# A fused attention and feed-forward block: x and x1 transposed by DVE after loads in 128-byte pieces, and score masks written as products of steps

## The chip, the core and the metric

The kernel runs on one core of a Trainium2 chip. TensorE (PE, with its weight loads shown apart as PEld), VectorE (DVE), ScalarE (ACT) and GpSimd (POOL) each run their own instruction list in order. SyncE (SP) issues nearly all transfers, in order too, and waits for the semaphores of each before it issues it. The metric is the device time of one execution in microseconds; the profiled execution gives a span, from the first instruction to the last, which is a little shorter than its time.

## What is computed

One block with the norm behind each part: x is 4096 rows of 256 values in fp32, `x1 = norm(x + attention(x))`, `out = norm(x1 + ffn(x1))`. Attention has 16 heads of 16 values in 4 groups that share keys and values, and a row sees itself and the 127 rows before it:

```python
scores = einsum('bghqd,bgkd->bghqk', q, k) / sqrt(16)
mask   = (i - 128 >= j) | (i < j)
att    = softmax(where(mask, -1e9, scores));  out = att @ v @ Wo + bo
# ffn, with x_prev = the row before
xr = mu_r * x + (1 - mu_r) * x_prev;  xk = mu_k * x + (1 - mu_k) * x_prev
out = sigmoid(xr @ W_r.T) * (square(relu(xk @ W_k.T)) @ W_v.T)
```

## The kernel before

The 4096 rows are cut into blocks of 128, pairs of blocks (p = 0 to 15, 256 rows each) and chunks of two pairs (c = 0 to 7, 512 rows).

**How the order is made.** Every stage is an operation given to `op(...)` with its kind, what it reads and writes, which buffers of a ring (a pool of a few tiles in turn) and which of the eight PSUM banks it takes. The table `KINDS` gives each kind its engine, an assumed length in microseconds and a rank. `Plan.run` then plays the operations through: each engine takes, among the operations that could start within a small window (`WAIT`, for PE `PE_WAIT`), the one of lowest rank plus `base`, which is about its pair's number. A change of the way that PE is cut into tiles (`mode`) is charged `TURN`; a transfer is counted as landed `LAND` after SP has issued it. The instructions of all engines are written out in the order that comes of this, so it is fixed when the program runs.

**The stages of a pair.**

- `plan_load` loads x of a pair (256 KB, 1 KB rows, ring of 4). `plan_xT` transposes it on PE by four 128x128 transposes (L560) and ACT copies the result from PSUM (L567).
- `plan_kv`, `plan_q` (per chunk; L583, L631) make kT and qT, each head group with spare rows beside its 16 values. `q move` (L653) is four transfers inside SBUF that shift half of qT, in pieces of 128 bytes; `ones` (L617) fills the spare row of kT. `plan_v` transposes the values (L606) and DVE copies them (L611).
- `plan_maxima`, in three units: first scores on PE with their masks (L695, L708), their negated maxima by DVE (L718), a small DVE transpose (L728), and `nm put` (L732), four transfers of 4 KB that place the maxima in the spare row of qT.
- `plan_weights_a` (per block) and `plan_weights_b` (per pair): second scores on PE, transposed, so that keys lie on partitions, with the maxima already subtracted (L787); before them their masks (L775); then exp by ACT (L827, L855). `half_scores` and `scores` build these. The masks are matmuls of a shifted identity (`intoE`, `intoO`, cut out of `identZ`) with `maskOwn`, `maskPrev` or, for the block before the first, `maskNone`. They set half of the 64 rows at a time: one half by a mask of one group of columns, the other half by a mask of two.
- `plan_values` (L882, L895) multiplies by the values; DVE turns, scales and turns back (L907 to L927).
- `plan_out`: xres is x loaded again (L1006) with bo added by POOL (L1012), `wo` on PE (L1021), the sum by DVE (L1031), then the norm: `stats` on DVE (L960), `scale` on POOL (L966 to L972), `apply` on ACT (L978). The result is x1 (ring of 6).
- `plan_x1T` transposes x1 on PE (L1054) and ACT copies it (L1067) into x1T, one column further right, the first column being the last of the pair before (L1064, POOL).
- `plan_mix`: POOL takes differences of neighbouring columns (xd, L1082), DVE mixes (xm, L1090). `plan_k`, `plan_r`, `plan_vout`: products fk (L1118), fr and fv (L1144), relu and tanh on ACT, square (L1132) and the sum with x1 (L1176) on POOL, the gate (L1171) on DVE, then the second norm and the store (L1182). The last pair ends in half pairs (`plan_last`).

`load_rest`, one operation, loads W_r, W_k, W_v, Wo and bo; the three W are transposed by PE once (`plan_weight`).

Of the kernel before, what the change touches and what calls it, by code (L numbers as in the profile page):

```python
# [20 lines left out]
P = 128  # L21
# [13 lines left out]
    "w": (PE, 0.43, -14.24),  # L35
    "w copy": (ACT, 0.62, 3.74),
    "x load": (SP, 0.5, -8.79),
    "x first": (SP, 3.3, -12.27),
    "x second": (SP, 2.5, -8.28),
    "xT": (PE, 0.43, 0.69),  # L40
    "xT copy": (ACT, 0.6, 5.02),
    "kv": (PE, 1.72, -6.04),
    "kv copy": (ACT, 0.69, -12.31),
    "vT": (PE, 0.43, -3.72),
    "vT copy": (DVE, 0.4, 1.8),
    "ones": (SP, 0.1, -12.06),
    "q": (PE, 1.72, -2.77),
    "q copy": (ACT, 0.69, -9.26),
    "q move": (SP, 2.0, -9.27),
    "maxima": (PE, 0.93, -1.84),  # L50
    "maxima 2": (PE, 0.66, -2.01),
    "reduce": (DVE, 1.14, 1.56),
    "reduce 2": (DVE, 0.81, -16.65),
    "nm turn": (DVE, 0.21, -6.03),
    "nm put": (SP, 2.0, 5.46),
    "weights a": (PE, 1.1, -0.52),
    "exp a": (ACT, 1.02, -9.82),
    "weights b": (PE, 1.3, -0.14),
    "exp b": (ACT, 1.02, 8.26),
    "values": (PE, 2.7, 0.67),  # L60
    "oN": (DVE, 1.25, -2.26),
    "rs": (DVE, 0.35, 9.56),
    "at": (DVE, 0.9, -0.26),
    "attT": (DVE, 0.44, 3.73),
    "xres": (SP, 0.5, -7.25),
    "bo": (POOL, 1.3, 19.18),
    "wo": (PE, 1.72, 2.61),
    "y": (DVE, 0.69, 9.88),
    "x1T first": (POOL, 0.25, 21.46),
    "x1T": (PE, 0.43, 3.16),  # L70
    "x1T copy": (ACT, 0.6, 10.29),
    "xd": (POOL, 1.3, -1.75),
    "xm": (DVE, 0.45, 27.04),
    "fk": (PE, 1.72, 6.41),
    "relu": (ACT, 0.6, 4.81),
    "square": (POOL, 1.07, 27.6),
    "fr": (PE, 1.72, 7.15),
    "gate": (ACT, 0.6, 13.52),
    "fv last": (PE, 0.86, 37.29),
    "y2 last": (DVE, 0.42, 26.45),  # L80
    "stats last": (DVE, 1.0, 21.07),
    "scale last": (POOL, 1.05, -29.88),
    "apply last": (DVE, 0.46, -15.48),
    "fv": (PE, 1.72, 3.74),
    "y2": (DVE, 0.69, -0.64),
    "y2 add": (POOL, 1.3, -4.68),
    "store": (SP, 0.5, -2.34),
    "rest": (SP, 4.5, 9.89),
    "stats y": (DVE, 0.6, 9.58),
    "scale y": (POOL, 1.5, 16.27),  # L90
    "apply y": (ACT, 0.6, 3.08),
    "stats y2": (DVE, 0.6, 10.75),
    "scale y2": (POOL, 1.5, -23.39),
    "apply y2": (ACT, 0.6, 23.42),
# [46 lines left out]
class Plan:  # L141
# [7 lines left out]
    WAIT = 0.39  # L149
    PE_WAIT = 0.20  # L150
    TURN = 0.2

    def __init__(self):
        self.ops = []
        self.writer, self.readers = {}, {}
        self.users, self.taker = {}, {}
        self.banks = Banks()

    def op(self, kind, base, fn, r=(), w=(), uses=(), new=(), banks=(), mode=None):
# [5 lines left out]
        rank += base  # L165
# [19 lines left out]
        self.ops.append((eng, length, rank, fn, deps, list(new), list(banks), mode))  # L185

    def run(self):
# [40 lines left out]
        while cand:  # L228
            best = {}
            for i in cand:  # L230
                s = ring_time(i)
                if s is None:
                    continue
                e = ops[i][0]
                s = max(ready[i], s, free.get(e, 0.0))
                places = None
                if ops[i][6]:
                    found = self.banks.find([k for _, k in ops[i][6]], free_at, s)
                    if found is None:
                        continue  # L240
                    s, places = found
                turn = self.TURN if e == PE and ops[i][7] != last_mode else 0.0
                best.setdefault(e, []).append((s + turn, i, places))
# [8 lines left out]
            eng, length, _, fn, _, new, banks, mode = ops[i]  # L252
# [8 lines left out]
            land = eng == SP  # L261
            free[e] = s + length
            end[i] = s + (self.LAND + length if land else length)
            order.append((s, len(order), i))
            for k in nexts[i]:
                hop = 0.0 if ops[k][0] == eng and not land else self.DRAIN if eng == PE else self.HOP
# [13 lines left out]
def postln_block(  # L280
# [45 lines left out]
    small = ctx.enter_context(tc.tile_pool(name="small", bufs=2))  # L326
    psum = ctx.enter_context(tc.tile_pool(name="psum", bufs=1, space=PSUM))
# [21 lines left out]
    def load_x(p):  # L349
# [4 lines left out]
        )  # L354

# [122 lines left out]
    identZ = const.tile([P, 3, Q], BF16, tag="identZ", name="identZ")  # L478
    nc.vector.memset(identZ, 0.0)
    nc.vector.tensor_copy(identZ[:, 1, :], identR[:, 0, :])  # L480
    intoE = identZ[:, 1:3, :].rearrange("p a b -> p (a b)")
    intoO = identZ[:, 0:2, :].rearrange("p a b -> p (a b)")


    nc.vector.tensor_tensor(diag, diag, after, ALU.add)
    four = diag.to_broadcast([P, GS, Q])
    maskOwn = const.tile([P, 2, GS, Q], BF16, tag="maskOwn", name="maskOwn")
    maskPrev = const.tile([P, 2, GS, Q], BF16, tag="maskPrev", name="maskPrev")
    nc.vector.memset(maskOwn[:, 0, :, :], NEG)
    nc.vector.memset(maskPrev[:, 1, :, :], NEG)  # L490
    nc.vector.tensor_scalar(maskOwn[:, 1, :, :], four, -NEG, NEG, ALU.mult, ALU.add)
    nc.vector.tensor_scalar(maskPrev[:, 0, :, :], four, NEG, None, ALU.mult)
    maskNone = const.tile([P, T], BF16, tag="maskNone", name="maskNone")
    nc.vector.memset(maskNone, NEG)
# [17 lines left out]
    def load_rest():  # L512
        for k, w in (("r", W_r), ("k", W_k), ("v", W_v)):
            load_w(ffn_l[k], w)
        for g in range(NG):
            nc.sync.dma_start(
                out=wo[32 * g : 32 * (g + 1), :, :],
                in_=Wo[64 * g : 64 * (g + 1), :].rearrange("(rp x) n -> x rp n", x=32),
            )
        nc.sync.dma_start(out=bo_b, in_=bo.partition_broadcast(P))  # L520
# [4 lines left out]
    def plan_weight(k, base, scale):  # L525
# [14 lines left out]
        op("w", base, turn, r=["rest"], w=[("wps", k)], banks=[(key, 1)], mode="full")  # L540
# [5 lines left out]
    def plan_load(p):  # L546
        if p > 1:
            op("x load", p, lambda: load_x(p), w=[("x", p)], new=[(ring("x", 4), ("x", p))])
# [3 lines left out]
    def plan_xT(p, base):  # L552
# [18 lines left out]

        op("xT", base, turn, r=[("x", p)], w=[key + ("ps",)], uses=[("x", p)] + ([("xTt", c)] if h else []),
# [184 lines left out]
    def scores(b, h, dst, own, r0, nr, first):  # L757

        c, blk = divmod(b, NB)
        k0 = (b + own) * P + 64 * h  # L760
        RQ = GS * Q
        if own:
            lo = (2 * h - r0) * RQ
            masks = ((intoE, maskOwn[:, 1:2], lo, 1), (intoO, maskOwn[:, 0:2], lo, 2))
        elif b == 0:
            masks = ((intoE, None, 0, nr), (intoO, None, 0, nr))
        else:
            lo = (2 * h - r0) * RQ
            masks = ((intoE, maskPrev[:, 0:2], lo, 2), (intoO, maskPrev[:, 0:1], lo + RQ, 1))

        def mask(i):
            into, m, lo, n = masks[i]
            for g in range(NG):
                q = slice(32 * g, 32 * (g + 1))
                nc.tensor.matmul(  # L775
                    dst[g][:, lo : lo + n * RQ],
                    into[q, :],
                    maskNone[q, 0 : n * RQ] if m is None else m[q].rearrange("p s r i -> p (s r i)"),
                    start=(i == 0 and first),
                    stop=False,  # L780
                    skip_group_check=True,
                )

        def product():
            for g in range(NG):
                k = slice(32 * g, 32 * g + DH + 1)
                nc.tensor.matmul(  # L787
                    dst[g],
                    kT[k, k0 : k0 + 64],
                    qT[c][k, blk, r0 : r0 + nr, :, :].rearrange("p s r i -> p (s r i)"),  # L790
                    start=False,
                    stop=True,
                    skip_group_check=True,
                )

        return mask, product

    def half_scores(b, sc, cols, kinds, first):
        parts = []
        for h in range(2):  # L800
            own, r0, nr = kinds[h]
            dst = [
                sc[g // 2][64 * h : 64 * (h + 1), g % 2, cols] for g in range(NG)
            ]
            parts.append(scores(b, h, dst, own, r0, nr, first))
        for i in range(2):
            for mask, _ in parts:
                mask(i)
        for _, product in parts:
            product()  # L810
# [6 lines left out]
    def plan_weights_a(b, base):  # L817
# [3 lines left out]
        def product():  # L821
            half_scores(b, [two_banks(k) for k in keys], slice(0, T), ((1, 0, NS), (0, 0, NS)), True)
# [14 lines left out]
    def plan_weights_b(p, base):  # L837
# [3 lines left out]
        def product():  # L841
            sc = [two_banks(k) for k in keys]
            for j in range(2):
                half_scores(
                    2 * p + j,
                    sc,
# [481 lines left out]
```

## Time and profile before

| | us |
|---|---|
| median of three runs | 356.84 (355.78 to 358.21) |
| the profiled execution | 357.12 |
| its span | 355.4 |
| DVE: maxima reduce (L718), 96 | 94.0 |
| DVE: mixing (L1090), 64 | 34.3 |
| ACT: exp (L827 and L855), 96 | 92.9 |
| ACT: copies of x1T and xT (L1067, L567), 32 | 18.2 |
| PE: transposes of x (L560), 64, and of x1 (L1054), 64 | 9.2 and 10.3 |
| PE: masks of second scores (L775), 1024 | 70.2, overlapping |

The busy time of a group is what its own instructions cover. PE runs several small matmuls side by side in parts of its array, so groups overlap and their times are not to be added up; the price of a stage is better read from the starts of the stages, one after the other. The rest of what matters is shown with the prediction.

### The profile page before, as it was taken

To read this page: it belongs to the slowest core of one execution; us is meant where nothing else is said; L and a number is where in the kernel's file an instruction comes from. 1 tells how busy PE (TensorE), PEld (TensorE's weight loads), DVE (VectorE), ACT (ScalarE), POOL (GpSimd) and SP (SyncE) were. 2 spreads that over 40 slices of the span, in tenths; PEclk is the share of its full clock that TensorE was granted. 3 is DMA by queue.
4 is the path that set the end of the run, shared out by engine and by line. 5 is a ranking of instruction groups with operands and counts; after the bars stand their busy time and mean duration, and the time that the engine had idled before them with its cause. 6 is when DMAs were issued, how large, how long until landed. Compare 5 with 4: busy or idle time off the path is not lost.

```text
span 355.4 us, 11751 instructions
## 1 busy us (share of the span) xinstructions
PE 342.9 (96%) x5091; PEld 230.2 (65%) x5091; DVE 244.8 (69%) x464; ACT 179.0 (50%) x253; POOL 125.8 (35%) x223
## 2 busy tenths in 40 slices
PE   6999999999999999999999999999999999999982
PEld 5655565566747676767657676766757676667871
DVE  4146474888593898988927987388845888548554
ACT  3423537273537284647355554737456373863441
POOL 5110000412234363534315251253505352626883
PEclk9989999999999999999999999999999999999997
DMA  6855150140004101102223020320205020200011
GB/s 187 260 88 77 50 92 5 32 64 5 8 29 34 61 33 33 50 16 58 66 21 73 5 61 5 31 61 4 63 3 83 16 60 5 61 4 0 31 59 60
DMA packets 34518, 17.34 MB, mean 49 GB/s; under 512 B 20734, under 2 KB 34434, under 8 KB 34466
## 3 DMA queue, kind: packets, MB, share of 16 engines
q1 hardware_dynamic: 34288, 16.46, 20.5%
q8 instruction: 40, 0.66, 0.8%
q10 hardware_dynamic: 178, 0.13, 0.1%
q14 instruction: 12, 0.10, 0.1%
HBM read 9.97 MB, written 4.19 MB: 40 GB/s over the span
## 4 chain that ended last, share of the span: by engine, by line
PE 91%; DMA 3%; DVE 2%; ACT 1%; SPq 1%; POOL 1%; issue 1%; POOLq 0%; DVEq 0%; ACTq 0%
PE ps L1144 15%; PE ps L787 13%; PE ps L708 10%; PE ps L882 9%; PE ps L1021 8%; PE ps L631 8%; PE ps L1118 7%; PE ps L895 5%; PE ps L775 4%; PE ps L583 4%; PE ps L1054 3%; PE ps L695 2%; PE ps L560 2%; PE ps L606 1%; DMA qT<-qT 1%; DMA x<-in_L_attn_x 1%
## 5 line engine op out<-in xcount | busy, mean ns | idle before, releaser
L718 DVE TENSOR_REDUCE nm<-ps 128x6 f32<-128x960 f32 (+1 forms) x96 | 94.0, 1034 | 21.3 <-PE ps L708 20.9
L827 ACT ACTIVATE prA<-ps 128x1024 f32<-128x1024 f32 x64 | 61.7, 1023 | 38.1 <-PE ps L787 35.2
L787 PE MATMUL ps<-qT,kT 17*64 17x256 f32 (+1 forms) x1024 | 57.6, 495 | 0.0
L708 PE MATMUL ps<-kT,qT 16*128 16x160 f32 x1024 | 46.0, 305 | 0.4 <-DMA qT<-qT 0.4
L1176 POOL TENSOR_TENSOR y<-y,x 128x512 f32<-128x512 f32 x15 | 20.9, 1394 | 59.3 <-DVE y L1171 59.3
L708 PEld LDWEIGHTS ps<-kT,qT 16*128 16x128 f32 x1024 | 37.4, 185 | 2.7 <-issue 1.3
L966 POOL TENSOR_SCALAR ve_y<-mv_y 128x2 f32<-128x2 f32 x31 | 8.0, 257 | 87.6 <-DVE mv_y L961 87.3
L1090 DVE SCALAR_TENSOR_TENSOR xm<-xd,vecs,x1T 128x256 f32<-128x256 f32 x64 | 34.3, 582 | 1.4 <-POOL xd L1082 1.4
L855 ACT ACTIVATE prB<-ps 128x1024 f32<-128x1024 f32 x32 | 31.2, 1034 | 3.8 <-PE ps L787 3.8
L631 PE MATMUL ps<-xT,wq 128*128 128x512 f32 x64 | 32.4, 631 | 0.0
L1021 PE MATMUL ps<-wo,attT 128*128 128x256 f32 x128 | 31.6, 389 | 0.0
L882 PE MATMUL ps<-prA,vA 128*32 128x256 f32 x512 | 30.9, 382 | 0.6 <-DVE nm L718 0.6
L960 DVE BATCH_NORM_STATS2 st_y<-y 128x6 f32<-128x256 f32 x62 | 25.3, 408 | 8.7 <-POOL y L1176 8.2
L1082 POOL TENSOR_TENSOR xd<-x1T 128x512 f32<-128x512 f32 x16 | 16.6, 1041 | 40.6 <-ACT x1T L1067 40.6
L775 PEld LDWEIGHTS <-identZ 32*64 32x64 bf16 x1024 | 18.2, 104 | 19.5 <-issue 18.5
L1118 PE MATMUL ps<-xm,wkT 128*128 128x256 f32 x128 | 30.3, 380 | 0.3 <-ACT prB L855 0.3
L1144 PE MATMUL ps<-wrT,xm 128*128 128x256 f32 x128 | 30.4, 380 | 0.0
L1144 PE MATMUL ps<-wvT,kact 128*128 128x256 f32 x120 | 29.4, 387 | 0.8 <-ACT sig L1158 0.8
L1144 PEld LDWEIGHTS ps<-wvT,kact 128*128 128x128 f32 x120 | 22.0, 190 | 11.6 <-issue 7.5
L1012 POOL TENSOR_TENSOR xres<-xres,bo_b 128x512 f32<-128x512 f32 x16 | 20.4, 1278 | 25.2 <-DMA xres<-in_L_attn_x 13.7
L1021 PEld LDWEIGHTS ps<-wo,attT 128*128 128x128 f32 x128 | 23.2, 190 | 7.9 <-ACT prA L827 5.3
L1031 DVE TENSOR_TENSOR y<-ps,xres 128x512 f32<-128x512 f32 x16 | 11.1, 691 | 23.0 <-PE ps L1021 17.5
(99 smaller groups left out, 511.3 us busy)
## 6 DMA issues: line engine op xcount, KB each, us to landing
x<-in_L_attn_x SPq DMA_DIRECT2D x16, 256.0 KB
xres<-in_L_attn_x SPq DMA_DIRECT2D x16, 256.0 KB
out<-res SPq DMA_DIRECT2D x15, 256.0 KB
qT<-qT SPq DMA_DIRECT2D x32, 64.0 KB
qT<-nmT SPq DMA_DIRECT2D x64, 4.0 KB
wl_xk<-in_L_attn_Wq SPq DMA_DIRECT2D x1, 256.0 KB
wl_xr<-in_L_ffn_W_r SPq DMA_DIRECT2D x1, 256.0 KB
wl_xr<-in_L_ffn_W_k SPq DMA_DIRECT2D x1, 256.0 KB
```

Source lines behind the costliest of these rows:

```text
L631: nc.tensor.matmul(ps, wq[:, ch, rp, :, :].rearrange("p g x -> p (g x)"), xT[c][:, ch, :], start=(ch == 0), stop=(ch == C2 - 1),)
L708: nc.tensor.matmul(sc[g // 2][:, g % 2, u * W : (u + 1) * W], qT[c][g0 : g0 + DH, (2 * p + j) % NB, s, :, :].rearrange("p r i -> p (r i)") ...
L718: nc.vector.tensor_reduce(nms[p % 2].rearrange("p g j s -> p g (j s)")[:, 2 * i : 2 * i + 2, lo:hi], two_banks(keys[i])[:, :, 0 : n * W].r ...
L775: nc.tensor.matmul(dst[g][:, lo : lo + n * RQ], into[q, :], maskNone[q, 0 : n * RQ] if m is None else m[q].rearrange("p s r i -> p (s r i) ...
L787: nc.tensor.matmul(dst[g], kT[k, k0 : k0 + 64], qT[c][k, blk, r0 : r0 + nr, :, :].rearrange("p s r i -> p (s r i)"), start=False, stop=Tru ...
L827: nc.scalar.activation(prA[b][:, 2 * i : 2 * i + 2, :], two_banks(keys[i]), AF.Exp)
L855: nc.scalar.activation(prB[p][:, 2 * i : 2 * i + 2, :, :].rearrange("p g j n -> p g (j n)"), two_banks(keys[i]), AF.Exp,)
L882: nc.tensor.matmul(av[32 * g : 32 * (g + 1), hf, j, :], vA[:, values_of(b, g)], prA[b][:, g, hf * H : (hf + 1) * H], start=(j == 0), stop= ...
L1021: nc.tensor.matmul(ps[:, j, :], attT[2 * p + j][:, rp, :, :].rearrange("p s i -> p (s i)"), wo[:, rp, :], start=(rp == 0), stop=(rp == 1),)
L1090: nc.vector.scalar_tensor_tensor(dst[p][:, ch, :], st["d"][:, ch, :], muT[:, which, ch : ch + 1], x1T[p][:, ch, 0:H2], ALU.mult, ALU.add,)
L1118: nc.tensor.matmul(ps[:, o, :], ffnT["k"][:, ch, o * P : (o + 1) * P], xk[p][:, ch, :], start=(ch == 0), stop=(ch == C2 - 1),)
L1144: nc.tensor.matmul(ps[:, b, :], lhs[:, ch, b * P : (b + 1) * P], w[:, ch, :], start=(ch == 0), stop=(ch == C2 - 1),)
```

## The change

1. **x.** For pairs 4 to 15 x is no longer loaded in rows. Four transfers a pair (`load_x_turned`, `turned_rows`), each an operation of its own, put every 32x32 block of x, as it is, at the place that its transpose belongs to; a piece is 32 values, 128 bytes. One DVE transpose of 128x512, which transposes each 32x32 block in place (`x turn`), then gives xT. Pairs 0 to 3 keep PE and ACT.
2. **x1.** For pairs 0 to 13 x1 is written to memory (`x1 out`), read back by four such transfers (`x1 in`) and turned by DVE (`x1 turn`) into x1T. The last two pairs keep PE and ACT.
3. **Masks of the second scores.** The masks are products of a step (`step` or its complement `back`, shifted by a choice of columns) with a row `negR` that is the same for all groups of columns. Each half is now set by a mask of one group of columns (`put_masks`); in `plan_weights_b` one matmul covers both blocks of the pair, and all masks come ahead of all products.
4. **The plan.** Ranks and some lengths in `KINDS` are new; `ADJUST` adds a rank of its own to each PE operation; a transfer in pieces is counted as landed after `LAND_PIECES`; `mode` "32x64" after itself is charged `DRY`; `WAIT` is smaller. `rest` becomes five operations, in the order k, r, v, bo, wo, and each user waits for its own.

```diff
+    def turned_rows(a, dst, rows):
+        src = rows.rearrange("(b i) (c a j) -> a i c b j", i=Q, c=C2, j=Q)
+        with nc.allow_non_contiguous_dma(reason="rows of 32"):
+            nc.sync.dma_start(
+                out=dst[32 * a : 32 * (a + 1), :, :].rearrange("p c (b j) -> p c b j", j=Q),
+                in_=src[a],
+            )
...
+        if p > 3:
+            for a in range(4):
+                op("x load", p, lambda a=a: load_x_turned(p, a), w=[("x", p, a)], uses=[("x", p)] if a else [],
+                   new=[] if a else [(ring("x", 4), ("x", p))])
...
+        def squares():
+            if c not in xT:
+                xT[c] = sb.tile([P, C2, T], F32, tag="xT", name=f"xT_{c}")
+            nc.vector.transpose(xT[c][:, :, h * 2 * P : (h + 1) * 2 * P], xs[p])
+
+        if c > 1:
+            op("x turn", base, squares, r=[("x", p, a) for a in range(4)], w=[key], uses=[("x", p)] + ([("xTt", c)] if h else []),
+               new=[] if h else [(ring("xT"), ("xTt", c))])
+            return
...
+    def put_masks(dst, own, first, second, start=(True, True)):
...
+        for i, (part, cols) in enumerate(((FIRST, first), (SECOND, second))):
+            for h in range(len(dst)):
+                for g in range(len(dst[h])):
+                    q = slice(32 * g, 32 * (g + 1))
+                    d = dst[h][g][:, :, cols[h] : cols[h] + RQ]
+                    nc.tensor.matmul(
+                        d,
+                        flat(step if own[h] else back)[q, part],
+                        negR[q, 0 : d.shape[1], :, :].rearrange("p s r i -> p (s r i)"),
...
-            half_scores(b, [two_banks(k) for k in keys], slice(0, T), ((1, 0, NS), (0, 0, NS)), True)
+            sc = [two_banks(k) for k in keys]
+            dst = [[sc[g // 2][64 * h : 64 * (h + 1), g % 2, :] for g in range(NG)] for h in range(2)]
+            if b:
+                put_masks(
+                    [[d.rearrange("p (o n) -> p o n", o=1) for d in half] for half in dst],
+                    (True, False), (0, 2 * RQ), (RQ, 3 * RQ),
+                )
...
+            if p:
+                put_masks(dst, (False, True), (0, 0), (RQ, RQ))
...
+        def out_():
+            x1d[p] = dram.tile([2 * P, D], F32, tag="x1d", name=f"x1d_{p}", bufs=4)
+            nc.sync.dma_start(out=x1d[p].rearrange("(b p) d -> p b d", p=P), in_=x1[p])
...
+        if p < NP - 2:
+            op("x1 out", base, out_, r=[("x1", p, 0), ("x1", p, 1)], w=[("x1d", p)], uses=[("x1t", p)], new=[(ring("x1d", 4), ("x1dt", p))])
+            for a in range(4):
+                op("x1 in", base, lambda a=a: in_(a), r=[("x1d", p)], w=[("x1w", p, a)], uses=[("x1dt", p)] + ([("x1wt", p)] if a else []),
+                   new=[] if a else [(ring("x1w"), ("x1wt", p))])
+            op("x1 turn", base, squares, r=[("x1w", p, a) for a in range(4)] + [("x1T0", p)], w=[key], uses=[("x1wt", p), ("x1Tt", p)])
+            return
...
-            op("rest", 0, load_rest, w=["rest"])
+            for k in ("k", "r", "v", "bo", "wo"):
+                op("rest" if k in ffn_l else "rest " + k, 0, lambda k=k: load_rest(k), w=[("rest", k)])
```

## The prediction

> **What bounds the kernel now.** I read the page's head and busy rows first, then its slices, then the busy times by stretch, and last the timelines of single engines over one period of the steady state.
>
> ```profile
> span 355.4 us, 11751 instructions
> PE 342.9 (96%) x5091; PEld 230.2 (65%) x5091; DVE 244.8 (69%) x464; ACT 179.0 (50%) x253; POOL 125.8 (35%) x223
> ...
> PE   6999999999999999999999999999999999999982
> ...
> PE 91%; DMA 3%; DVE 2%; ACT 1%; SPq 1%; POOL 1%; issue 1%; POOLq 0%; DVEq 0%; ACTq 0%
> ```
>
> TensorE is busy 96% of the span and carries 91% of the chain that ended last. Only the first and last few microseconds have holes.
>
> ```profile
> core 0: us, PE busy (x) PEld busy (x) DVE busy (x) ACT busy (x) POOL busy (x), PEclk, DMA share, GB/s
> ...
> 213.73:255.14 41.41, 41.41 (x634) 27.93 (x633) 29.95 (x55) 22.13 (x31) 14.88 (x26) 1.00 0.17 35
> ```
>
> One period of two pairs (256 rows each) takes 41.41 us and PE is busy for all of it, at full granted clock. DVE has 11.5 us free in it, ACT 19, and the DMA share is 0.17. In this stretch PE work that disappears shortens the period one for one, until something else is late.
>
> Where in PE's timeline the removed and changed work sits (start, duration, line, shape, count):
>
> ```profile
> 213.57 1.04 PE L560 MATMUL ps<-ident,x 128*128 128x128 f32 x8
> 214.44 1.89 PE L1144 MATMUL ps<-wrT,xm 128*128 128x256 f32 x8
> ...
> 237.06 0.66 PE L1054 MATMUL ps<-ident,x 128*128 128x128 f32 x4
> 237.56 1.89 PE L1144 MATMUL ps<-wrT,xm 128*128 128x256 f32 x8
> ...
> 242.48 0.25 PE L775 MATMUL ps<-maskOwn,identZ 32*64 32x128 bf16 x4
> ...
> 242.67 1.04 PE L787 MATMUL ps<-qT,kT 17*64 17x512 f32 x16
> 243.53 0.28 PE L775 MATMUL ps<-maskPrev,identZ 32*64 32x256 bf16 x4
> ...
> 245.08 1.99 PE L1021 MATMUL ps<-wo,attT 128*128 128x256 f32 x8
> ```
>
> Durations overlap, so the price of a step is the distance between starts: 8 x transposes cost 214.44 - 213.57 = 0.87 (0.435 a pair); four x1 transposes 237.56 - 237.06 = 0.50, of which about 0.07 is the change of stage that stays. "weights a" takes 243.53 - 242.48 = 1.05, its masks 0.19 of it; "weights b" takes 245.08 - 243.53 = 1.55.
>
> **The change, part by part.**
>
> *Transposes off PE.* x of pairs 4 to 15 (12) and x1 of pairs 0 to 13 (14) lose their PE transposes: 26 x 0.43 = 11.2 us, all on the path. ACT loses 26 copies of 0.59 us (its rows L567 and L1067), 15.3 us; ACT waits for PE in its largest waits, so that is room, not time.
>
> *The same work on DVE.* 26 transposes of 128x512 f32. The trace has 1245 ns for 128x1024 (oN) and 424 for 128x256 (attT); in between 0.70, in all 18.2 us. DVE's period goes from 29.95 to 29.95 + 4 x 0.70 = 32.75 of about 39, or 84%. Its longest hole is a wait of 4.08 us for PE's L1144, so there is cover; I count nothing. With the cover gone, each turn delays the maxima's reduce behind it on DVE, which holds PSUM banks that PE waits for: up to 18.2.
>
> *The transfers.* A turned x is four DMAs of 512 pieces of 128 bytes; x1 adds one plain 256 KB write to memory and four such reads. The nearest row is the q move: four DMAs, the same pieces, SBUF to SBUF.
>
> ```profile
> 215.84 2.24 SPq L732 DMA_DIRECT2D qT<-nmT  x4
> ...
> 224.15 3.24 SPq L653 DMA_DIRECT2D qT<-qT  x4
> ...
> 232.52 0.39 SPq L1182 DMA_DIRECT2D out<-res  x1
> ```
> ```profile
> 226.00:226.50 0.50, 0.50 (x33) 0.49 (x31) 0.00 (x0) 0.05 (x1) 0.48 (x1) 1.00 0.75 61
> ```
>
> Issue takes SP 3.24 us; data moves from 225.4 to 229.5, 4.2 us at 61 GB/s, so 5.4 us from first issue to the end. SP's period now has about 9.9 us of issue; four turned groups add 13.0 and two x1 writes 0.8: 23.7 of 39. The DMA engines' period becomes 4.2 (q move) + 2 x (4.2 x + 4.2 x1 + 1.4 each for the x1 write, xres and the store, from the 208 to 210.5 stretch of the same table) = 29.4, or 75%, so it fits.
>
> [...] The row is SBUF to SBUF, but these pieces come from memory. [...] One row has small pieces from memory, Wk's 64 KB in 256-byte pieces, which moves alone just before DVE copies it at 4.85:
>
> ```profile
> 4.50:5.00 0.50, 0.50 (x5) 0.50 (x4) 0.15 (x1) 0.50 (x1) 0.50 (x1) 1.00 0.27 64
> ```
>
> 0.27 x 16 engines x 0.5 us over 125 pieces (64 GB/s for 0.5 us) is 17 ns of an engine a piece; the q move's row gives 0.75 x 16 x 0.5 over 238, 25 ns. Memory pieces are no dearer than the q move's here, so I take the q move's price: it fits, cost 0. [...]
>
> *Latency of the round trip.* x1 is normalised by ACT at 234.33; today PE transposes at 237.06, xd starts at 238.42, the first fk of that pair runs at 246.91. New: 234.33 + 2.5 (a store: 208.53 to about 210.5, plus landing) + 5.9 (the q move's 5.4, and landing) + 0.70 = 243.4, xd 1.04, two xm of 0.58: 245.6, still before 246.9. What is late by more has six x1 buffers to run a period later. The last two pairs keep the PE path, so the tail chain is not lengthened.
>
> *Waits on SP.* The x1 write waits for ACT, the reads for the write's landing; behind them on SP stand nm put, xres, q move and stores. The nm put is the tight one: issued 215.84 to 218.08, its packets end near 219.0, "weights a" starts at 220.13. Slack is about 1.1 us. Its order on SP is planned, with 0.75 us per piece group; I cost it at 0 and keep 0.8 us x 14 = 11 as upper end. Order changed by the new ranks and the ADJUST lists can also gain: PE's stage changes cost 0.1 to 0.25 each (1.29, 1.18 and 1.05 for one and the same "weights a") with some eight a pair. No row says what a new order saves; 0 to 8 us, and I set it equal to stalls of about 2, net 0.
>
> *Masks.* In "weights a" each PSUM tile gets 256 mask columns instead of 384 with the same 16 matmuls: 0.19 becomes 0.13, 32 x 0.06 = 1.9 us (from 0, if the issue limits, to 0.12 each). In "weights b" 32 mask matmuls in two waves (0.17 each up to the first score) become 16 in one, 768 columns a tile become 512: 0.10 to 0.2 saved, 16 x 0.15 = 2.4. Sum 4.3, range 2 to 7.
>
> *Start.* DVE loses about 1.7 us of mask building and gains about 1.0; the first user runs at 39.2 and the removed ops end at 9.2. Splitting "rest" into five operations reorders loads that land long before use. Zero each; without cover, under 1 us.
>
> *Sum.* 11.2 + 4.3 = 15.5. Span 355.4 gives 339.9. The profiled execution took 357.12, 1.7 more than its span, and lies 0.3 above the median 356.84: 339.9 + 1.7 - 0.3 = 341.3. I say 340.5, as the masks may give a little more.
>
> **The rivals.**
>
> 1. *DMA engines become the bound* (slower, 0.08). Place: the ring that x, x1, q move, nm put and stores share. Price per period 12.6 + 16.8 f, with f the price of a memory piece over the q move row; the saving is gone at f = (41.4 - 12.6) / 16.8 = 1.7, from there it is slower. At f = 2: 46.2 - 41.4 = 4.8 for six periods, less 5 saved in the two with few pieces: about 380. [...] Against: 75% at the row's rate, Wk's 17 ns, and x loads can run four buffers ahead.
>
> 2. *A DVE that is too full* (within 1%, 0.07). All 26 turns delay a reduce: 340.5 + 18 = 358. For it: the slices show DVE at 9 in a third of the span already. Against: the 4.08 us hole every period, and 84%.
>
> 3. *nm put behind the pieces* (0.17). DMA takes 4.2 us for what SP issues in 3.24: after a group the ring is about 1 us behind, the size of nm put's slack. 14 x 0.8 = 11: 346 to 353, middle 350.
>
> 4. *The new order also removes stage changes* (0.08): 6 to 10 us more, 332.
>
> 5. That the change does not move PE work can be excluded by its code: for those pairs no PE transpose is issued.
>
> **How the numbers follow.** The likeliest case (0.60) gives 340.5, with 334 to 347 from the masks' range and small stalls. Cases 1 and 2 lie above 353.3. Runs here spread by 0.7%, so a change under about 1% can't be told from none. Faster: 0.60 + 0.17 + 0.08 = 0.85; same 0.07; slower 0.08. The range 331 to 354 leaves out case 1, most of case 2, and a tail below 331: under 2 in 10.
>
> **What would show it.** After: PE busy near 327 with holes still only at the ends; no L560-like transposes after the fourth pair; the period near 39; DVE near 263; ACT near 164. Case 1 shows a DMA share near 1 and PE waiting for xm or x turns; case 2 PE waiting for DVE reduces; case 3 weights waiting for DMA qT<-nmT. I am wrong if piece reads land later than about 6 us after first issue, or if PE's busy time falls while its holes grow by as much.

## The result and the profile after

The changed kernel takes 358.31 us (median of 20 runs, 356.22 to 364.42); the kernel before, run beside it, takes 357.54 (355.23 to 359.01). The ratio is 1.0028, 95% interval 1.0005 to 1.0052: no gain, where 340.5 was forecast. Two of the twenty, at 361.70 and 364.42 us, lie over 1.5% above the fastest and are left out of the ratio.

The page of the changed kernel shows, in this order, the span, the busy times, two rows of its slices, the packets of the main DMA queue and the chain's shares.

```profile
span 356.2 us, 11173 instructions
...
PE 334.6 (94%) x4739; PEld 211.4 (59%) x4739; DVE 265.7 (75%) x487; ACT 165.8 (47%) x227; POOL 128.6 (36%) x223
...
PE   6996988999999999999999999999999999999982
...
PEclk9996996999999999999999999999999999999997
...
q1 hardware_dynamic: 89744, 23.80, 31.1%
...
PE 67%; DVE 14%; DMA 5%; issue 3%; ACT 3%; SPq 3%; POOL 2%; POOLq 0%; DVEq 0%; ACTq 0%
```

The work went where it was sent: DVE 265.7 (forecast 263), ACT 165.8 (164), and a turn on DVE costs what was estimated (0.70):

```profile
L1199 DVE STREAM_TRANSPOSE x1T<-x1w 128x512 f32<-128x512 f32 x14 | 9.8, 702 | 1.5 <-DMA x1w<-x1d 1.5
```

But PE's busy time fell by 8.3 us, not by 15.5, and its holes (span less busy) grew from 12.5 to 21.6. PE's row dips at the fourth, sixth and seventh slice, the clock's at the fourth and seventh. Before, PE was at 9 there, and the clock's only dip ahead of the end was one 8, at the third:

```profile
PEclk9989999999999999999999999999999999999997
```

The busy times by stretch say where the time went. I cut each span at the start of the second and of the sixteenth values stage (both kernels run 16). The kernel before comes first, then the changed one. After the length come the busy times of PE, PEld, DVE, ACT and POOL with their counts, then granted clock, DMA share and GB/s.

```profile
0.00:64.50 64.50, 60.61 (x743) 37.67 (x743) 31.56 (x68) 28.17 (x41) 8.20 (x23) 0.97 0.47 109
64.50:318.70 254.20, 253.66 (x4172) 169.27 (x4169) 191.27 (x340) 138.59 (x190) 94.13 (x161) 1.00 0.16 35
318.70:355.40 36.70, 28.66 (x185) 23.21 (x184) 21.94 (x57) 12.25 (x22) 23.50 (x41) 0.95 0.11 37
```
```profile
0.00:74.60 74.60, 64.58 (x759) 36.80 (x760) 38.29 (x75) 26.54 (x37) 9.62 (x24) 0.91 0.49 94
74.60:324.10 249.50, 246.06 (x3821) 156.06 (x3821) 207.91 (x364) 127.97 (x170) 98.48 (x164) 1.00 0.30 65
324.10:356.20 32.10, 24.01 (x161) 18.54 (x160) 19.52 (x50) 11.34 (x21) 20.52 (x36) 0.94 0.12 41
```

The middle is 4.7 us shorter and the end 4.6 us; the start is 10.1 us longer and takes it all back. In the start PE's holes grow from 3.9 to 10.0 us, and the granted clock falls from 0.97 to 0.91. PE's view of waits names two for DMA that are new (us in total, how often, the longest):

```profile
PE ps L619 <- DMA wl_xr<-in_L_ffn_W_r: 2.9, 1, 2.9
PE ps L619 <- DMA wl_kact<-in_L_ffn_W_v: 2.0, 1, 2.0
```

SP's timeline shows why W_r is late (start, length of the issue, line, transfer, count), and the chain that ended last shows what it took from there:

```profile
25.03 0.59 SPq L436 DMA_DIRECT2D x<-in_L_attn_x  x1
25.67 0.63 SPq L455 DMA_DIRECT2D wl_xr<-in_L_ffn_W_r  x1
26.34 1.94 SPq L436 DMA_DIRECT2D x<-in_L_attn_x  x3
```
```profile
25.67 4.75 DMA wl_xr<-in_L_ffn_W_r
30.47 1.11 PE ps L619 x4
31.58 5.28 PE ps L731 x8
```

In the kernel before, W_r and W_v are issued at 8.65 and 9.67 us, and Wo behind them at 10.18. Now the five parts of "rest" have places of their own in SP's order: W_r stands among transfers in pieces at 25.67 and lands 4.75 us later, W_v is issued at 51.29, Wo at 59.37. Before, then after:

```profile
8.65 0.46 SPq L370 DMA_DIRECT2D wl_xr<-in_L_ffn_W_r  x1
9.67 0.47 SPq L370 DMA_DIRECT2D wl_kact<-in_L_ffn_W_v  x1
```
```profile
51.29 0.43 SPq L455 DMA_DIRECT2D wl_kact<-in_L_ffn_W_v  x1
59.37 0.62 SPq L602 DMA_DIRECT2D wo<-in_L_attn_Wo  x1
```

The plan counts a W transfer as landed 1.4 + `LAND` 2.0 = 3.4 us after its start and puts PE's user right there or soon after. For W_r that is 1.4 us too short. W_v did land in 3.3 us (PE's wait ends at 54.63), but SP had fallen behind its plan: when `Plan.run` is played through, W_r comes 11.6 us and W_v 32.2 us after W_k, while on the chip they came 16.3 and 41.9 us after it. Around the first wait the clock falls too:

```profile
26.00:28.00 2.00, 1.29 (x24) 0.82 (x16) 1.97 (x2) 0.00 (x0) 0.00 (x0) 1.00 0.83 114
28.00:30.00 2.00, 0.00 (x0) 0.00 (x0) 2.00 (x4) 0.00 (x0) 0.00 (x0) 0.59 0.92 166
30.00:32.00 2.00, 1.53 (x5) 1.25 (x6) 1.96 (x4) 0.38 (x1) 0.00 (x0) 0.50 0.48 76
32.00:34.00 2.00, 2.00 (x4) 0.74 (x3) 0.51 (x1) 0.21 (x1) 0.00 (x0) 0.50 0.61 95
34.00:36.00 2.00, 2.00 (x5) 0.96 (x4) 0.00 (x0) 0.69 (x1) 0.00 (x0) 0.71 0.04 6
```

PE waits from 27.6 to 30.5; the granted clock (third number from the right) is halved from 28.34 to 35.17, most of it after the wait. Another such half-clock stretch runs from 55.65 to 62.48, after the wait for W_v. Each lasts 6.83 us. In the second, four matmuls of L683 took 3.78 us from 57.29 on, against 1.88 from 43.58 on at whole clock. So PE loses half of the time that it works in such a stretch: 3.4 us in the second, but only 2.3 in the first, since PE stands idle in 2.1 us of that one. The kernel before has one stretch, of 3.41 us, at 24.04, and loses 1.7 (both kernels have a last stretch, from 352.61 and from 351.72 us to the end, in which PE is busy for 0.00 us). So the start's 10.1 us are, to 0.1, 6.1 of holes and 4.1 of clock (5.8 against 1.7).

### The profile page after: what moved, and what is told of

Its sections match the earlier page's. It is cut to its first block, busy times and chain, and to the rows that moved or that the text cites. A ratio compares the mean times of both kernels' runs of the same rounds, so it can differ in the third digit from the quotient of the medians.

```text
span 356.2 us, 11173 instructions
## 1 busy us (share of the span) xinstructions
PE 334.6 (94%) x4739; PEld 211.4 (59%) x4739; DVE 265.7 (75%) x487; ACT 165.8 (47%) x227; POOL 128.6 (36%) x223
## 4 chain that ended last, share of the span: by engine, by line
PE 67%; DVE 14%; DMA 5%; issue 3%; ACT 3%; SPq 3%; POOL 2%; POOLq 0%; DVEq 0%; ACTq 0%
PE ps L896 10%; PE ps L1279 10%; PE ps L731 7%; PE ps L1137 7%; PE ps L997 7%; PE ps L1253 7%; PE ps L808 5%; DVE nm L818 5%; PE ps L1010 4%; PE ps L683 4%; PE ps L868 3%; DVE xm L1225 3%; ACT prA L933 1%; SPq L753 1%; DMA wl_xr<-in_L_ffn_W_r 1%
## 5 line engine op out<-in xcount | busy, mean ns | idle before, releaser
L896 PE MATMUL ps<-qT,kT 17*64 17x512 f32 (+1 forms) x1024 | 53.1, 494 | 0.0
L808 PE MATMUL ps<-kT,qT 16*128 16x160 f32 x1024 | 46.9, 307 | 0.7 <-DMA qT<-qT 0.7
L808 PEld LDWEIGHTS ps<-kT,qT 16*128 16x128 f32 x1024 | 38.2, 188 | 2.0 <-DMA qT<-qT 1.2
L1225 DVE SCALAR_TENSOR_TENSOR xm<-xd,vecs,x1T 128x256 f32<-128x256 f32 x64 | 36.0, 610 | 1.2 <-POOL xd L1217 1.2
L1093 ACT ACTIVATE res<-y,nmr_y,rstd_y 128x256 f32<-128x256 f32 x30 | 16.5, 594 | 29.0 <-POOL nmr_y L1087 28.9
L1253 PEld LDWEIGHTS ps<-xm,wkT 128*128 128x128 f32 x128 | 23.3, 190 | 10.2 <-issue 2.6
L1022 DVE STREAM_TRANSPOSE oN<-ps 128x1024 f32<-128x1024 f32 x16 | 19.8, 1240 | 11.3 <-PE ps L1010 7.7
L1279 PEld LDWEIGHTS ps<-wrT,xm 128*128 128x128 f32 x128 | 23.7, 190 | 6.4 <-issue 1.4
L1093 ACT ACTIVATE x<-y,nmr_y,rstd_y 128x256 f32<-128x256 f32 x32 | 17.4, 596 | 19.0 <-POOL nmr_y L1087 16.8
```

What stands on the lines that cost most here:

```text
L808: nc.tensor.matmul(sc[g // 2][:, g % 2, u * W : (u + 1) * W], qT[c][g0 : g0 + DH, (2 * p + j) % NB, s, :, :].rearrange("p r i -> p (r i)") ...
L896: nc.tensor.matmul(dst[g], kT[k, k0 : k0 + 64], qT[c][k, blk, r0 : r0 + nr, :, :].rearrange("p s r i -> p (s r i)"), start=False, stop=Tru ...
L1093: nc.scalar.activation(dst()[:, b, :], src()[:, b, :], AF.Identity, bias=st["nmr"][:, b : b + 1], scale=st["rstd"][:, b : b + 1],)
L1225: nc.vector.scalar_tensor_tensor(dst[p][:, ch, :], st["d"][:, ch, :], muT[:, which, ch : ch + 1], x1T[p][:, ch, 0:H2], ALU.mult, ALU.add,)
L1253: nc.tensor.matmul(ps[:, o, :], ffnT["k"][:, ch, o * P : (o + 1) * P], xk[p][:, ch, :], start=(ch == 0), stop=(ch == C2 - 1),)
L1279: nc.tensor.matmul(ps[:, b, :], lhs[:, ch, b * P : (b + 1) * P], w[:, ch, :], start=(ch == 0), stop=(ch == C2 - 1),)
```

## The experiments

All ratios are to the kernel before, run beside, with 95% intervals. My theory was that the place of the weight loads on SP costs the start. Its rivals were the pieces themselves (DMA bound or slow to issue), a DVE that is too full, and masks or an order that give nothing.

**W_r and W_v issued with W_k.** In `load_rest`:

```
-        if k in ffn_l:
-            load_w(ffn_l[k], {"r": W_r, "k": W_k, "v": W_v}[k])
+        if k == "k":
+            for n, w in (("k", W_k), ("r", W_r), ("v", W_v)):
+                load_w(ffn_l[n], w)
+        elif k in ffn_l:
+            pass
```

> The changed kernel with the loads of W_r and W_v issued right behind that of W_k (9.4 us) instead of at 25.7 and 51.3 us; every engine's order stays as it is. Theory A (the two weight loads stand too late in SP's order, PE waits 2.9 and 2.0 us for them and then runs at half clock for some 5 us each time): both waits gone, the granted clock between 28 and 36 and between 55 and 62 us at 1.0 instead of 0.5, 8 to 11 us less than the changed kernel, so about 347 to 350 and a ratio to the kernel before of 0.97 to 0.98. Theory B (the pieces fill the DMA engines and everything at the start comes late): the waits move to other loads, less than 3 us gained. Theory C (DVE is the bound): no gain at the end, the time made good at the start is lost to DVE by 120 us.

354.83 us, ratio 0.9874 (0.9813 to 0.9935). Both waits are gone and the kernel is faster than before, but a third weight has become late, as its SP timeline, PE timeline and windows show:

```profile
48.91 6.72 SPq L436 DMA_DIRECT2D x<-in_L_attn_x  x10
55.68 3.09 SPq L605 DMA_DIRECT2D wo<-in_L_attn_Wo  x4
```
```profile
60.58 2.57 PE L1140 MATMUL ps<-wo,attT 128*128 128x256 f32 x8 [2.00 <-DMA wo<-in_L_attn_Wo]
```
```profile
60.00:62.00 2.00, 1.42 (x6) 1.32 (x7) 1.13 (x2) 0.00 (x0) 0.00 (x0) 0.95 0.04 9
62.00:64.00 2.00, 2.00 (x27) 0.81 (x34) 0.70 (x2) 0.00 (x0) 0.00 (x0) 0.50 0.23 36
64.00:66.00 2.00, 2.00 (x17) 0.50 (x2) 1.09 (x4) 0.67 (x1) 0.67 (x3) 0.50 0.65 123
```

Ten transfers in pieces ahead of Wo take SP 6.72 us; PE waits 2.0 us and a half-clock stretch of 6.83 us follows. The 347 to 350 us that were expected are missed by this.

**All weights early, and Wo in the middle.** With the edit above, Wo's four transfers too go to `k == "k"`; or, in the second kernel, to where W_v stood (`elif k == "v":`).

> The changed kernel with W_r, W_v and Wo all issued right behind W_k; the order of every engine stays. With W_r and W_v alone early, PE's next long wait was 2.0 us for Wo, and the half clock came behind that one instead. Theory A (weight loads late in SP's order, each wait of 2 us or more followed by 6.8 us at half clock): no wait of PE above 1 us after 20 us, no half-clock stretch of 6.8 us, 7 to 10 us under the changed kernel: 348 to 351, ratio 0.975 to 0.983. Theory B (pieces make everything at the start late): a further load takes over as the wait, 353 or more.

> The changed kernel with W_r and W_v issued behind W_k and Wo issued where W_v stood (about 49 us, ahead of ten groups of pieces, 9 us before its user); all orders stay. With Wo early too, the first q move took 7.4 us to land beside it and a 3.4 us half-clock stretch came there. Theory A (each load late or in another's way costs its wait and a half-clock stretch): neither that stretch nor Wo's wait of 2.0 us; 355 - 2.0 - 3.4 = 349.5, ratio 0.978. If a half-clock stretch comes at the start whatever the order: 351 to 353, as with all weights early.

352.85 us, 0.9885 (0.9842 to 0.9929), and 350.52, 0.9817 (0.9777 to 0.9857), where 348 to 351 and 349.5 were expected. With all of them first, no weight is waited for, but the first q move, issued at 15.05 just behind them, holds PE twice for half a microsecond up to 22.40. With Wo in the middle these two waits fall from 1.0 to 0.7 us together. Both profiles lose 1.7 us to one half-clock stretch of 3.41 us (at 24.25, and at 8.93), so the stretch that was to go away has moved; the intervals of the two overlap, and what makes the second faster, if it is, stays open. The stretches of `wo_at_v`:

```profile
0.00:67.20 67.20, 61.17 (x762) 35.51 (x763) 38.33 (x76) 26.52 (x37) 8.28 (x23) 0.97 0.56 102
67.20:316.70 249.50, 246.09 (x3824) 156.01 (x3826) 207.95 (x364) 127.94 (x170) 99.61 (x165) 1.00 0.29 66
316.70:348.80 32.10, 23.98 (x161) 18.51 (x160) 19.47 (x49) 11.35 (x21) 20.47 (x36) 0.97 0.12 41
```

Middle and end are those of the changed kernel to 0.1 us; the start is 7.4 us shorter, with the clock back at 0.97. This version has the lowest median of all: 1.8%, or some 6.5 us, below the kernel before run beside it (350.52 / 0.9817 = 357.05).

**The kernel before, with one weight late.** W_v leaves `load_rest` and is issued in `move()` of the first chunk, ahead of its four transfers, or behind them:

```
-        for k, w in (("r", W_r), ("k", W_k), ("v", W_v)):
+        for k, w in (("r", W_r), ("k", W_k)):
...
+            if c == 0:
+                load_w(ffn_l["v"], W_v)
```

> The kernel before with W_v's load alone issued later, just ahead of the first q move at about 15.9 us, so that PE stands idle some 2 us before it transposes W_v at about 17 us. If an idle PE costs only its wait: 2 us more, ratio 1.006. If the clock is halved for some 5 us after such a wait, as it looks in the changed kernel: 4 to 5 us more, ratio 1.012, and the granted clock is 0.5 in the stretch behind it.

> The kernel before with W_v's load alone issued behind the first q move (about 19.3 us) so that PE stands idle 4 us or more at about 17 us. If a long idle of PE costs its wait alone: 2 to 4 us more than before (part of it is a wait that came anyway behind it), granted clock 1.0. If it is followed by a half-clock stretch of 6.8 us: 3.4 us on top, 5 to 8 us more, ratio 1.015 to 1.022.

Ahead: 357.59 us, 1.0005 (0.9985 to 1.0025); PE waits 1.1 us for W_v, no half-clock stretch follows (even the one of the kernel before is missing; the mean clock of the profiled run is 0.996, against 0.990 there), and nothing is lost that can be measured, where 2 us or more were expected. Behind: 365.28, 1.0228 (1.0190 to 1.0265); PE waits 6.72 us and the clock is halved for 6.83 us, in part during the wait. PE's user of W_v, ahead and behind, then the windows of the second:

```profile
18.09 0.63 PE L532 MATMUL ps<-ident,wl_kact 128*128 128x128 f32 x4 [1.10 <-DMA wl_kact<-in_L_ffn_W_v]
```
```profile
25.25 1.09 PE L532 MATMUL ps<-ident,wl_kact 128*128 128x128 f32 x4 [6.72 <-DMA wl_kact<-in_L_ffn_W_v]
```
```profile
20.00:24.00 4.00, 0.00 (x0) 0.00 (x0) 0.00 (x0) 0.00 (x0) 0.00 (x0) 0.83 0.77 112
24.00:28.00 4.00, 2.75 (x7) 1.75 (x8) 0.00 (x0) 1.07 (x2) 0.00 (x0) 0.50 0.41 134
28.00:32.00 4.00, 4.00 (x30) 1.73 (x29) 0.00 (x0) 1.26 (x2) 0.00 (x0) 0.82 0.01 4
```

So one late weight, with no other part of the change present, makes the kernel 2.3% slower: of the 8.1 us by which its span is longer, 7.0 are PE's holes and 2.1 the clock, less 1.0 elsewhere.

**Rows in place of pieces.** The body of `turned_rows` moves the same 64 KB in 2 KB rows, in the changed kernel and in the one with all weights early; the order of instructions stays.

```
-        src = rows.rearrange("(b i) (c a j) -> a i c b j", i=Q, c=C2, j=Q)
-                in_=src[a],
+            in_=rows[64 * a : 64 * (a + 1), :].rearrange("(i b) d -> i (b d)", b=2),
```

> The changed kernel with each group of 128-byte pieces replaced by a transfer of the same 64 KB in 2 KB rows, so x and x1 are not put in transposed blocks and the output is of other numbers; order and DVE turns stay. Theory A (place in the order): W_r still waits most of what it did, since it is issued at the same place; 1 to 4 us gained, mostly at W_r's landing (4.75 us after issue now, near 3 then). Theory B (pieces fill the DMA engines): both waits gone, 8 us or more gained. Theory C (DVE): nothing gained after 100 us.

> As all_w_early, and each group of 128-byte pieces replaced by 64 KB in 2 KB rows (x and x1 then are not in transposed blocks, the output is of other numbers). What is left of the pieces' own price once no weight waits behind them: theory A 0 to 1 us less than all_w_early; theory B 4 us or more less.

351.06 us, 0.9828 (0.9767 to 0.9889), and 351.28, 0.9834 (0.9798 to 0.9870). In the late order rows save 7.3 us: PE's waits for W_r and W_v shrink to 0.4 and 0.7 us. That is more than the 1 to 4 us that I had allowed if the place alone were to blame: the late place costs what it does because of the pieces around it, and moving the loads or leaving out the pieces mends it equally. With the weights early rows save 1.6 us (352.85 to 351.28), which the intervals don't tell from nothing, and `wo_at_v`, with pieces, is as fast as either. Pieces thus show a cost only as what stands ahead of a weight on SP and on the DMA engines. The middle is 249.4 us long with rows and 249.5 with pieces in the late order, and 249.8 with both when all weights are early. What the pieces take there, SP's timeline and the DMA queue of the changed kernel show around four x1 reads (the queue from 110.8 to 116.5 us: packets, MB, share of 16 engines):

```profile
110.87 2.63 SPq L436 DMA_DIRECT2D x1w<-x1d  x4
```
```profile
q1 hardware_dynamic: 2184, 0.27, 30.1%
```

**The turns on ACT.** In the kernel with all weights early, each of the two `nc.vector.transpose` becomes an `nc.scalar.copy`.

> As all_w_early, with the 26 DVE turns replaced by copies on ACT at the same place of the plan (blocks are then not transposed, the output is of other numbers). It takes 18 us off DVE and puts some 15 us on ACT. If DVE is the next bound (in the changed kernel PE loses about 6 us between 80 and 290 us, mostly with DVE busy nine tenths): 3 to 6 us less than all_w_early. If not: within 1 us of it, or slower by delayed exps.

355.52 us, 0.9944 (0.9920 to 0.9967). The middle stays at 249.55 us (249.8 with the turns on DVE) although DVE is relieved of 26 turns; the start is longer, with another wait (1.6 us) and two half-clock stretches (mean clock 0.981, against 0.992). So DVE's turns do not bound the middle, unless the copies on ACT happen to cost the same.

**The masks alone** in the kernel before (`step`, `back`, `negR`, `put_masks`, `put_all` and `put_scores` of the change, nothing else), in the old order:

> The kernel before with the new masks of the second scores alone; its plan, its order and all else stay. The prediction's own price: 4.3 us less (2 to 7), ratio 0.988. If the spacing seen in the changed kernel (1.11 for 1.29 in weights a, 1.22 for 1.49 in weights b) is the masks' doing: 32 x 0.18 + 16 x 0.27 = 10 us less, ratio 0.972. If column count and issue do not matter: no change.

356.44 us, 0.9962 (0.9940 to 0.9984). The second scores with their masks, summed from start to start of PE's stages, fall from 62.5 to 59.4 us. Without the idle time behind them they fall from 62.4 to 58.8, so 3.6 us of the forecast 4.3 are there as PE time; holes take part back (span less PE busy 12.5 before, 13.9 here).

**Three of four transposes left out** in the kernel before, in the 26 stages that the change moves (here those of x), and the same with the new masks:

```
-            for ch in range(C2):
-                for b in range(2):
+            for ch in range(C2 if c < 2 else 1):
+                for b in range(2 if c < 2 else 1):
```

> The kernel before with three of the four PE transposes left out for x of pairs 4 to 15 and x1 of pairs 0 to 13 (ACT copies the one that is left four times, so the output is of other numbers); no transfer, no turn on DVE and no order is changed. It takes 78 x 0.108 = 8.4 us off PE. If PE time off the steady state shortens the run one for one, as the prediction held: 349, ratio 0.9765. If DVE, POOL or a ring takes over at once: 4 us or less gained, ratio above 0.988.

> As before_cut, with the new masks of the second scores as well. Both parts of the change that take work off PE, in the old order and without their transfers: if each gives what it gives alone, 8.4 + 1.1 to 3.1 us: 346 to 348, ratio 0.969 to 0.973. If the old order had no room for more: the same as before_cut.

353.58 us, 0.9884 (0.9803 to 0.9964), and 352.43, 0.9862 (0.9803 to 0.9921). The middle falls from 254.2 to 248.7 and 246.9. Both gain less than was expected (349 us, and 346 to 348), but not for want of PE time saved: with holes and half clock taken out, PE's time falls by 7.7 us in the first profile and 9.8 in the second, and the clock takes 4.8 and 3.4 us more than before. In the first kernel two of four runs took 351.4 us at a mean clock of 0.992 and two 355.8 at 0.975. The profile is of one of the latter and has two half-clock stretches of 6.83 us. The second stretch, from 49.6 us, has no long wait ahead of it:

```profile
48.00:50.00 2.00, 1.50 (x22) 1.21 (x26) 1.55 (x2) 2.00 (x4) 0.00 (x0) 0.89 0.74 61
50.00:52.00 2.00, 2.00 (x39) 1.92 (x36) 1.15 (x2) 0.09 (x1) 0.00 (x0) 0.50 0.84 96
52.00:54.00 2.00, 2.00 (x28) 0.98 (x24) 2.00 (x3) 0.00 (x0) 0.00 (x0) 0.50 0.76 243
```

**Order alone.** In the kernel before one number of the plan is changed, so that changes of PE's tiling are not charged:

```
-    TURN = 0.2
+    TURN = 0.0
```

> The kernel before with one number changed: the plan charges 0 instead of 0.2 us for a change of PE's tiling (TURN). Same instructions, loads in the same places; by the emitted order PE passes 114 times between full-array stages and stages of small tiles instead of 98, as often as in the changed kernel. Theory A (the new order's extra changes cost PE time): in the changed kernel the first scores take 3 to 4 us more than before and the keys' stage 2 to 2.6 us more, counted by the spacing of starts; here the same groups should grow together by 3 to 6 us, PE's busy time stay near 343, and the kernel be 0.8 to 1.7% slower. Theory B (those us come from the pieces or from DVE's turns, which this kernel does not have): first scores and keys stay within 1 us of before, ratio within 0.5% of 1.

376.43 us, 1.0556 (1.0523 to 1.0589), far more than either theory said. First scores and keys together grow by 5.8 us from start to start, as theory A expected, but not for its reason: without the idle time behind them the first scores take 42.3 us before and 42.6 here. PE's holes grow from 12.5 to 25.9 us. The page:

```profile
span 373.0 us, 11738 instructions
...
PE 347.1 (93%) x5091; PEld 226.8 (61%) x5091; DVE 247.9 (66%) x464; ACT 179.8 (48%) x253; POOL 126.5 (34%) x223
```

Theory A, that a change of tiling has a price of its own, is thus not shown; that an order by itself moves this kernel by over 5% is.

## Why the prediction was wrong

The step that failed is *Start*: "Splitting 'rest' into five operations reorders loads that land long before use. Zero each; without cover, under 1 us." The loads do not land long before use. W_r, W_v and Wo were moved on SP behind transfers in pieces, 17 to 49 us later than before, and the plan put their users where its own landing time, for W_r 1.4 us too short, and its own pace of SP, which the chip did not keep, let them. The cost was about 10 us, of which 7.4 came back when only these loads were moved.

A second step is *Order*, "net 0". With the loads put right (`wo_at_v`) only 6.5 of the 15.5 us are gained: what was to be saved was saved, and 5.1 us of holes and 4.4 us of PE time in stages that the change was not to touch were added. That the new order did this is likely and not shown.

Point by point:

- *Transposes off PE*, 11.2 forecast. From start to start, the transposes of x and x1 take 17.2 us before and 5.3 after: 12.0, or 12.4 without idle time. Right.
- *Masks*, 4.3 forecast. 3.6 as PE time in the old order, 3.1 with the holes behind; in the changed order 3.8 as PE time, 1.9 with holes and with the half clock. Right as work, and eaten in part. (The 70.2 us that the table of before gives for the masks are not in its trace: the matmuls of L775 cover 26.0.)
- *Turns on DVE, zero*. 0.70 us each; the middle does not change when they leave DVE. Right, and rival 2 falls as a mechanism, though the time it named (358) is the one that came: luck.
- *Transfers, zero* and rival 1. The four x1 reads at 110.87 us take SP 2.63 us, and the queue's 2184 packets take 30.1% of 16 engines for 5.7 us, so 12.6 ns each, half of the q move's 25. With f near 0.5, rival 1 is out: in the middle pieces cost nothing that can be seen (249.5 us with them, 249.4 with rows). At the start they were not free: rows saved 7.3 us in the late order. No run shows the doubled price (f = 2) from which rival 1's 380 was worked out; small pieces from memory were the cheaper ones here, 12.6 ns against 25.
- *Waits on SP*. Rival 3 looked at the right queue and at the wrong victim: `nm put` does not stand among PE's waits for DMA, the weights do.
- *Order, "net 0"*. The middle's holes went from 0.5 us to 3.4, with waits for DVE's maxima and ACT's exp, none over 0.7 us. They stay when pieces, turns and weight loads are put right. Over a third of the rise comes without the new order: with the new masks alone the middle has 1.3 us of holes, with masks and cut transposes 1.6. The rest is left to the order; the last experiment shows that order can do as much, though the changed order itself was not tried without the rest.
- *The clock* was not in the sum at all: it lost 5.8 us in the changed kernel and 1.7 before, where both were taken to be at full clock.

The balance against before, with each stage taken from start to start and its idle time and half clock counted apart: transposes 12.4 and second scores 3.8 us saved; 9.1 of holes, 4.1 of clock and 3.9 of PE time in other stages spent. That is the 0.8 us by which the span is longer. In `wo_at_v` 5.1 us of holes and 4.4 of such PE time stay between the 16.1 saved and the 6.6 by which its span is shorter. The PE time is spread over the first scores, the keys' and q's products and the products with the weights, 0.5 to 0.8 us each; in `before_masks` the first scores rise by 0.8 in the old order too. Why these stages take longer stays open. The forecast's own condition for being wrong, that busy time falls while holes grow as much, is what came.

## What to carry to other kernels

When a change splits or re-ranks loads, list each load's new issue time, what stands ahead of it on its queue and its first user; "lands long before use" is to be worked out for each, above all where the planner's landing time is shorter than a measured one, or where its queue runs behind the plan. A wait of PE of 2 to 3 us cost another 2.3 to 3.4 us of clock here, so price it at about twice its length. Take a saving of PE time in a plan that makes its own order as an upper bound: run the old work in another order to see how much order alone can move.

## What the runs showed of the hardware

But for the one at each kernel's end, the half-clock stretches lasted 3.41 us (the kernel before, `all_w_early`, `wo_at_v`) or 6.83 (the changed kernel, `w_with_k`, `before_wv_behind_q`, `before_cut`). In the profiles of the two kernels their starts, that of the last one included, lie whole multiples of 3.413 us apart: 28.34, 55.65 and 352.61 us in the changed kernel (8 and 87 of them), 24.04 and 351.72 in the kernel before (96).

Waits of 2.0, 2.0 and 2.9 us went with stretches of 6.83 us, one of 1.1 us with none. The length of a wait does not tell all. In the 3.41 us ahead of the changed kernel's two stretches PE was busy for 2.37 (W_r) and 1.43 us (W_v), ahead of the one of the kernel before for 3.02; yet 3.41 us with 2.11 busy, from 4.45 us on in the changed kernel, had whole clock in them and in the 3.41 us behind them. What decides stays open: in the profile of `before_cut` the stretch from 49.6 us has no long wait ahead of it (PE is busy for 1.50 us of the 2.00 from 48.00 on), and two of that kernel's four runs show a mean clock of 0.992 where the other two show 0.975.

A weight of 256 KB in 1 KB rows took 4.75 us from issue to landing among transfers in pieces; the plan allowed 3.4.
